# A recurrence step: the gates' weighted sums on DVE, the candidate's products on GpSimd and sums on ACT, scaling and adding fused

## The chip, the cores and the metric

The kernel runs on one core of a Trainium2 chip. The metric is the device time of one execution in microseconds, lower is better. The core has five engines with instruction queues of their own, which meet through semaphores: TensorE (PE in the profile, with PEld for its weight loads), VectorE (DVE), ScalarE (ACT), GpSimd (POOL) and SyncE (SP), which issues the transfers. TensorE writes its results into PSUM; the other operands lie in SBUF.

## The reference

The whole program is a stack of four residual layers over x of (2, 512, 128), each a conditioning block and a feed-forward block. The change lies in one of them, the conditioning block of layer 1: a gated recurrent unit with attention over a context of 77 tokens, run over the 512 positions one after the other for both batches.

```python
def step(h, x_t):
    hid = jnp.broadcast_to(h[:, None, :], (Bn, Sn, Hn))
    combined = jnp.concatenate([hid, enc_hiddens], axis=2)
    score = jnp.tanh(jnp.einsum('bsk,kh->bsh', combined, W_att))
    score = jnp.einsum('bsh,h->bs', score, V_att[:, 0])
    attn = jax.nn.softmax(score, axis=-1)
    context = jnp.einsum('bs,bsh->bh', attn, enc_hiddens)
    inp = jnp.concatenate([x_t, context], axis=1)
    gz, gr, gh = jnp.split(inp @ Wi + b, 3, axis=1)
    rz, rr, rh = jnp.split(h @ Uh, 3, axis=1)
    z = jax.nn.sigmoid(gz + rz)
    r = jax.nn.sigmoid(gr + rr)
    hh = jnp.tanh(gh + r * rh)
    h_new = z * h + (1.0 - z) * hh
    return (h_new, h_new)
_, outs = jax.lax.scan(step, last_hidden, jnp.swapaxes(dec_seq, 0, 1))
```

There are three sums over the attention for each of the 128 hidden units: one for the gate z, one for the gate r and one for the candidate hh. Everything is float32, B = 2, S = 512, and the context has NC = 77 tokens.

## The kernel before

`l1_xcond` (line 570) computes the block. Hidden units lie on the 128 partitions. What doesn't depend on the state is made ahead of the loop: `gx` holds the inputs' part of the three gates for all positions, `stat` the context's part of the score, and `gc` the context tokens already multiplied by the three gates' weights, as (batch, gate, token), 2 x 3 x 77 on each partition. `hs` holds the states of all steps.

The loop over `s` (line 611) stands in a manual schedule: every engine gets its instructions in the order of the source, and the waits between engines are worked out from what is read and written. One step goes like this, each line for both batches:

- TensorE multiplies the state by the score's weights (`pu`, line 614) and by the gates' recurrent weights, which it adds to `pc` in PSUM (lines 615, 625, 626). Columns 0 to 5 of `pc` then hold z, r and the candidate of both batches, columns 6 and 7 the half of the candidate's recurrent part.
- DVE adds `pu` to `stat` (`x`, line 619), ACT takes the tanh (`th`, line 621), TensorE weighs it with `vrep`, so that each partition holds all 77 scores (line 623).
- DVE takes the negative maximum of the scores (`nm`, line 629), ACT the exponential with its sum (`e` and `se`, line 634; in the trace a second instruction reads the accumulator).
- DVE multiplies the three rows of `gc` by `e` (`pr`, line 635), 231 elements for each batch, inverts the sum (`ri`, line 637), sums all products over the tokens (`pre`, line 639, 462 elements to 6), scales by `ri` (line 640) and adds `pc` (line 641).
- ACT makes both gates by one tanh of half the argument (`zr`, line 643), then the candidate for each batch, where `pre` is the bias and the gate r the scale (`hh`, line 646).
- DVE turns z into `oz` and `zh` (lines 649 and 651), multiplies `zh` by the old state (line 652) and makes the new state, one operation a batch (line 654).

`gates_in` (line 603) starts the next step's `pc` on TensorE with the inputs' part. GpSimd has no instruction in the loop.

Of the kernel before, what the change touches and what calls it, by code (L numbers as in the profile page):

```python
# [10 lines left out]
F32 = mybir.dt.float32  # L11
U8 = mybir.dt.uint8
AF = mybir.ActivationFunctionType
ALU = mybir.AluOpType
AX = mybir.AxisListType
PSUM = bass.MemoryType.PSUM

P = 128
B = 2
# [3 lines left out]
NC = 77  # L23
# [142 lines left out]
def tile_kernel(ctx: ExitStack, tc: tile.TileContext, d, off, out, phases=PHASES):  # L166
    nc = tc.nc
    pe, act, dve, pool = nc.tensor, nc.scalar, nc.vector, nc.gpsimd
# [27 lines left out]
    def mm_tile():  # L196
        return ps_tile("mm")
# [7 lines left out]
    def big(tag, bufs=None):  # L205
        t = act2[-1].tile([P, NT * P], F32, tag=tag, name=tag, bufs=bufs)
        return t
# [9 lines left out]
    def tview(t):  # L217
        return t.rearrange("p (t d) -> p t d", d=P)
# [12 lines left out]
    def col(name):  # L231
        a, n = off["cols"][name]
        return cols[:, a : a + n]
# [8 lines left out]
    def stage(*names):  # L242

        first = order.index(names[0])
        for k in order[:first]:
            weights.pop(k, None)
        load(order[: first + W_SLOTS])
        return parts(*names)
# [38 lines left out]
    def ln(src, dst, n=P, k=NT):  # L287

        st = sm([P, NT, 6], "ln_st")
        mv = sm([P, NT, 2], "ln_mv")  # L290
        for t in range(k):
            dve.bn_stats(st[:n, t, :], src[:n, t, :])
        for t in range(k):
            dve.bn_aggr(mv[:n, t, :], st[:n, t, :])
        r = rsqrt(mv[:n, :k, 1], n)
        for t in range(k):
            dve.tensor_scalar(dst[:n, t, :], src[:n, t, :], mv[:n, t, 0:1], r[:n, t : t + 1], ALU.subtract, ALU.mult)  # L297

    def transpose_to(dst, src, scale=None, bias=None):

        for b in range(B):
            ps = tr_tile()
            for i in range(TB):
                pe.transpose(ps[:, i * P : (i + 1) * P], src[:, b * TB + i, :], ident)
            o = dst[:, b * S : (b + 1) * S]
            if scale is None:
                act.copy(o, ps)
            elif bias is None:
                dve.tensor_scalar(o, ps, scale(b), None, ALU.mult)  # L309
            else:  # L310
                dve.tensor_scalar(o, ps, scale(b), bias(b), ALU.mult, ALU.add)

    def bcast(ap, shape, axis):
        return ap.unsqueeze(axis).to_broadcast(shape)
# [255 lines left out]
    def l1_xcond():  # L570
        w = stage("w1x")
        with tc.tile_pool(name="r1", bufs=1) as r1, tc.tile_pool(name="rs", bufs=3) as rs:
            y = tview(big("Y"))
            ln(X, y)
            yT = big("YT")
            transpose_to(yT, y)

            gx = r1.tile([P, S, 4, B], F32, tag="gx", name="gx")
            pool.memset(gx[:, :, 3, :], 0.0)
            for g in range(3):  # L580
                for b in range(B):
                    ps = mm_tile()
                    mm(ps, w("wi_x")[:, g * P : (g + 1) * P], yT[:, b * S : (b + 1) * S])
                    act.activation(gx[:, :, g, b], ps, AF.Identity, bias=col("gru_b")[:, g : g + 1])
            vrep = r1.tile([P, P], F32, tag="vrep", name="vrep")
            dve.tensor_copy(vrep, col("V_att").to_broadcast([P, P]))
            uhh = r1.tile([P, P], F32, tag="uhh", name="uhh")
            dve.tensor_scalar(uhh, w("uh")[:, 2 * P :], 0.5, None, ALU.mult)
            hs = r1.tile([P, S + 1, B], F32, tag="hs", name="hs")
            dve.tensor_copy(hs[:, 0, :], col("cond"))  # L590
            n2 = B * NC

            stat = r1.tile([P, B, NC], F32, tag="stat", name="stat")
            ps = mm_tile()
            mm(ps[:, :n2], w("wbot"), ctxT)
            act.copy(stat, ps[:, :n2].rearrange("p (b n) -> p b n", b=B))
            gc = r1.tile([P, B, 3, NC], F32, tag="gc", name="gc")
            for g in range(3):
                ps = mm_tile()
                mm(ps[:, :n2], w("wi_c")[:, g * P : (g + 1) * P], ctxT)  # L600
                act.copy(gc[:, :, g, :], ps[:, :n2].rearrange("p (b n) -> p b n", b=B))

            def gates_in(s):

                pc = o_tile()[:, :8]
                mm(pc, ident, gx[:, s].rearrange("p g b -> p (g b)"), start=True, stop=False)
                return pc

            with tc.manual_schedule():
                pc = gates_in(0)  # L610
                for s in range(S):
                    h = hs[:, s, :]
                    pu = mm_tile()[:, :B]
                    mm(pu, w("wtop"), h)
                    mm(pc[:, 0:2], w("uh")[:, :P], h, start=False, stop=False)
                    pb = []
                    for b in range(B):
                        x = rs.tile([P, NC], F32, tag="x", name="x")
                        dve.tensor_scalar(x, stat[:, b, :], pu[:, b : b + 1], None, ALU.add)  # L619
                        th = rs.tile([P, NC], F32, tag="th", name="th")  # L620
                        act.activation(th, x, AF.Tanh)  # L621
                        t = tr_tile()[:, :NC]
                        mm(t, vrep, th)
                        pb.append(t)
                    mm(pc[:, 2:4], w("uh")[:, P : 2 * P], h, start=False, stop=False)
                    mm(pc[:, 4:8].rearrange("p (c b) -> p c b", b=B), uhh, bcast(h, [P, 2, B], 1), start=False, stop=True)
                    nm = rs.tile([P, B], F32, tag="nm", name="nm")
                    for b in range(B):
                        dve.reduce_max(nm[:, b : b + 1], pb[b], axis=AX.X, negate=True)  # L629
                    e = rs.tile([P, B, NC], F32, tag="e", name="e")  # L630
                    se = rs.tile([P, B], F32, tag="se", name="se")
                    pr = rs.tile([P, B, 3, NC], F32, tag="pr", name="pr")
                    for b in range(B):
                        act.activation(e[:, b, :], pb[b], AF.Exp, bias=nm[:, b : b + 1], accum_out=se[:, b : b + 1])  # L634
                        dve.tensor_tensor(pr[:, b], gc[:, b], bcast(e[:, b, :], [P, 3, NC], 1), ALU.mult)  # L635
                    ri = rs.tile([P, B], F32, tag="ri", name="ri")
                    dve.reciprocal(ri, se)
                    pre = rs.tile([P, B, 3], F32, tag="pre", name="pre")
                    dve.tensor_reduce(pre, pr, AX.X, ALU.add)  # L639
                    dve.tensor_tensor(pre, pre, bcast(ri, [P, B, 3], 2), ALU.mult)  # L640
                    dve.tensor_tensor(pre, pc[:, 0:6].rearrange("p (g b) -> p b g", b=B), pre, ALU.add)  # L641
                    zr = rs.tile([P, B, 2], F32, tag="zr", name="zr")
                    act.activation(zr, pre[:, :, 0:2], AF.Tanh, scale=0.5)  # L643
                    hh = rs.tile([P, B], F32, tag="hh", name="hh")
                    for b in range(B):
                        act.activation(hh[:, b : b + 1], pc[:, 6 + b : 7 + b], AF.Tanh, bias=pre[:, b, 2:3], scale=zr[:, b, 1:2])  # L646
                    pcn = gates_in(s + 1) if s + 1 < S else None
                    oz = rs.tile([P, B], F32, tag="oz", name="oz")
                    dve.tensor_scalar(oz, zr[:, :, 0], -0.5, 0.5, ALU.mult, ALU.add)
                    zh = rs.tile([P, B], F32, tag="zh", name="zh")  # L650
                    dve.tensor_scalar(zh, zr[:, :, 0], 0.5, 0.5, ALU.mult, ALU.add)
                    dve.tensor_tensor(zh, zh, h, ALU.mult)
                    for b in range(B):
                        dve.scalar_tensor_tensor(hs[:, s + 1, b : b + 1], hh[:, b : b + 1], oz[:, b : b + 1], zh[:, b : b + 1], ALU.mult, ALU.add)  # L654
                    pc = pcn
            for b in range(B):
                ps = tr_tile()
                for i in range(TB):
                    pe.transpose(ps[:, i * P : (i + 1) * P], hs[:, 1 + i * P : 1 + (i + 1) * P, b], ident)
                ts_ = slice(b * TB, (b + 1) * TB)  # L660
                dve.tensor_tensor(X[:, ts_, :], X[:, ts_, :], tview(ps), ALU.add)
# [860 lines left out]
```

## Time and profile before

| What | Value |
|---|---|
| median of 3 runs | 6121.79 us |
| lowest and highest run | 6116.77 and 6127.82 us |
| the profiled execution: its own time | 6117.5 us |
| the profiled execution: its span | 6115.7 us |
| busy over the span: TensorE, DVE, ACT, POOL | 4296.3, 3110.0, 2092.1, 176.0 us |
| first and last `hs` of the loop start at | 265.5 and 3282.0 us |
| granted TensorE clock from 1000 to 2000 us | 0.50 |

The profile belongs to one execution. Its page has the span in equal slices, the chain that ended last and the costliest groups of instructions; the trace behind it can be asked for a stretch of time or for the instructions on one tile. In a row of the groups stand the line, the engine, the operation, the tiles as output and inputs, the shape and the count; after the bar the busy time in us and the mean duration in ns of one; after the second bar how long the engine was idle before these instructions, and who ended that. A line of a helper (215 is the helper of all matmuls) stands for many places, and then the tiles' names tell them apart.

### The profile page before, as it was taken

The page shows a single profiled execution, that of the slowest core. Times are in us where ns is not written, and L with a number is a line of the kernel's source. Part 1 is how long each engine was busy: PE and PEld are TensorE (multiplying, and loading weights), DVE is VectorE, ACT ScalarE, POOL GpSimd, SP SyncE. Part 2 cuts the span into 40 slices and gives each one's busy share as a digit, 9 for nine tenths or more (in the row PEclk, how much of TensorE's full clock was granted, in tenths as well). Part 3 has the DMA queues.
Part 4 walks back from the last instruction along what each step waited for, and adds up shares of the span by engine and source line. Part 5 has one row for each costly group of instructions (what it writes and reads, how often), then busy time and mean ns, then how long its engine had stood idle before and what let it go on. Part 6 is the DMA issues. An engine that isn't in the chain of part 4 may idle for free. (4 is left out here: it accounts for less than half of the span.)

```text
span 6115.7 us, 60242 instructions
## 1 busy us (share of the span) xinstructions
PE 4296.3 (70%) x19864; PEld 2898.0 (47%) x19864; DVE 3110.0 (51%) x10630; ACT 2092.1 (34%) x6050; POOL 176.0 (3%) x152
## 2 busy tenths in 40 slices
PE   4755555555555555555557999978888888888878
PEld 2655555555555555555555666833333333333334
DVE  6555555555555555555555444344444444444323
ACT  1433333333333333333333333314333333333322
POOL 2000000000000000000000000010000000000000
PEclk7855555555555555555556999779888888888866
DMA  1000000000000000000000000010000000000000
GB/s 37 26 1 1 1 1 1 1 0 1 1 1 1 1 0 1 1 1 1 1 1 15 21 1 5 1 42 7 6 18 6 18 6 18 6 20 7 7 4 6
DMA packets 15847, 44.43 MB, mean 7 GB/s; under 512 B 4179, under 2 KB 7965, under 8 KB 13869
## 3 DMA queue, kind: packets, MB, share of 16 engines
q1 hardware_dynamic: 15533, 40.57, 2.5%
q8 instruction: 157, 2.57, 0.2%
q14 instruction: 157, 1.29, 0.1%
HBM read 28.26 MB, written 0.52 MB: 5 GB/s over the span
## 5 line engine op out<-in xcount | busy, mean ns | idle before, releaser
L215 PE MATMUL mm<-hs,w1x 128*128 128x2 f32 x1024 | 299.9, 362 | 1204.2 <-DVE hs L654 1204.2
L215 PEld LDWEIGHTS mm<-hs,w1x 128*128 128x128 f32 x1024 | 255.9, 310 | 1252.5 <-DVE hs L654 1249.1
L1230 DVE TENSOR_REDUCE nm<-st 128x2 f32<-128x1024 f32 x384 | 462.5, 1223 | 418.1 <-PE st L215 417.6
L1236 ACT ACTIVATE pT<-st 128x1024 f32<-128x1024 f32 x384 | 389.0, 1023 | 815.2 <-PE st L215 794.7
L215 PE MATMUL tr<-th,vrep 128*128 128x77 f32 x2048 | 580.6, 436 | 120.1 <-ACT th L621 120.1
L215 PEld LDWEIGHTS o<-hs,w1x 128*128 128x128 f32 x2048 | 559.1, 333 | 0.0
L215 PEld LDWEIGHTS tr<-th,vrep 128*128 128x128 f32 x2048 | 473.9, 321 | 164.2 <-ACT th L621 164.2
L215 PE MATMUL o<-hs,w1x 128*128 128x2 f32 x2048 | 549.6, 338 | 0.0
L215 PE MATMUL st<-kp,qp 31*128 31x512 f32 (+1 forms) x1600 | 494.9, 751 | 71.9 <-DMA kp<-q 60.3
L629 DVE TENSOR_REDUCE nm<-tr 128x1 f32<-128x77 f32 x1024 | 243.4, 238 | 571.5 <-PE tr L215 571.5
L215 PE MATMUL st<-qp,kp 32*128 32x512 f32 (+1 forms) x1600 | 485.4, 710 | 39.9 <-DVE nm L1230 36.5
L634 ACT ACTIVATE e<-tr,nm 128x77 f32<-128x77 f32 x1024 | 333.6, 326 | 464.7 <-DVE nm L629 458.9
L621 ACT ACTIVATE th<-x 128x77 f32<-128x77 f32 x1024 | 226.4, 268 | 653.6 <-DVE x L619 653.6
L635 DVE TENSOR_TENSOR pr<-gc,e 128x231 f32<-128x231 f32 x1024 | 409.7, 400 | 43.1 <-ACT e L634 0.9
L619 DVE TENSOR_SCALAR x<-stat,mm 128x77 f32<-128x77 f32 x1024 | 225.3, 263 | 358.7 <-PE mm L215 358.7
L643 ACT ACTIVATE zr<-pre 128x4 f32<-128x4 f32 x512 | 105.6, 206 | 823.2 <-DVE pre L641 823.2
L639 DVE TENSOR_REDUCE pre<-pr 128x6 f32<-128x462 f32 x512 | 324.6, 634 | 0.0
L646 ACT ACTIVATE hh<-o,pre,zr 128x1 f32<-128x1 f32 x1024 | 303.9, 347 | 17.8 <-ACT zr L643 0.2
L215 PE MATMUL o<-gx,ident 128*128 128x8 f32 x1024 | 293.8, 361 | 0.0
L215 PE MATMUL acc<-pT,va 128*32 128x512 f32 (+1 forms) x1600 | 283.4, 685 | 12.8 <-ACT pT L1236 9.7
L215 PE MATMUL o<-hs,uhh 128*128 128x4 f32 x1024 | 290.5, 354 | 0.0
L215 PEld LDWEIGHTS st<-kp,qp 31*128 31x128 f32 (+1 forms) x1600 | 152.9, 219 | 275.5 <-issue 203.4
(361 smaller groups left out, 6145.5 us busy)
## 6 DMA issues: line engine op xcount, KB each, us to landing
w3x<-in_w3x SPq DMA_DIRECT2D x6, 1664.0 KB
qp<-q SPq DMA_DIRECT2D x104, 64.0 KB
kp<-q SPq DMA_DIRECT2D x48, 64.0 KB
w1g<-in_w1g SPq DMA_DIRECT2D x1, 2560.0 KB
w2a<-in_w2a SPq DMA_DIRECT2D x1, 2176.0 KB
w2b<-in_w2b SPq DMA_DIRECT2D x1, 2176.0 KB
w3f<-in_w3f SPq DMA_DIRECT2D x1, 1940.0 KB
w0g<-in_w0g SPq DMA_DIRECT2D x1, 1760.0 KB
```

The costliest lines, as they stand in the source:

```text
L215: pe.matmul(o, lhsT, rhs, start=start, stop=stop)
L619: dve.tensor_scalar(x, stat[:, b, :], pu[:, b : b + 1], None, ALU.add)
L621: act.activation(th, x, AF.Tanh)
L629: dve.reduce_max(nm[:, b : b + 1], pb[b], axis=AX.X, negate=True)
L634: act.activation(e[:, b, :], pb[b], AF.Exp, bias=nm[:, b : b + 1], accum_out=se[:, b : b + 1])
L635: dve.tensor_tensor(pr[:, b], gc[:, b], bcast(e[:, b, :], [P, 3, NC], 1), ALU.mult)
L639: dve.tensor_reduce(pre, pr, AX.X, ALU.add)
L643: act.activation(zr, pre[:, :, 0:2], AF.Tanh, scale=0.5)
L646: act.activation(hh[:, b : b + 1], pc[:, 6 + b : 7 + b], AF.Tanh, bias=pre[:, b, 2:3], scale=zr[:, b, 1:2])
L1230: dve.reduce_max(nms[h, g][:, j0 : j0 + 2, 0, u], ps, axis=AX.X, negate=True)
L1236: act.activation(pT, ps, AF.Exp)
```

## The change

`pr` holds two gates' products instead of three, so DVE multiplies 2 x 77 elements a batch and sums 308. The candidate's row of `gc` is multiplied by `e` on GpSimd into a tile of its own, `prc`, one instruction a batch, and ACT sums it by a copy onto itself with an accumulator (`sc`), one copy a batch, placed after both exponentials. Scaling and adding are one operation of DVE for each batch (times `ri`, plus `pc`), where they were two operations over both batches. The candidate's value gets an operation of the same kind in the loop over the batches that makes `hh`.

```diff
-                    pr = rs.tile([P, B, 3, NC], F32, tag="pr", name="pr")
+
+                    pr = rs.tile([P, B, 2, NC], F32, tag="pr", name="pr")
+                    prc = rs.tile([P, B, NC], F32, tag="prc", name="prc")
                     for b in range(B):
                         act.activation(e[:, b, :], pb[b], AF.Exp, bias=nm[:, b : b + 1], accum_out=se[:, b : b + 1])
-                        dve.tensor_tensor(pr[:, b], gc[:, b], bcast(e[:, b, :], [P, 3, NC], 1), ALU.mult)
+                        dve.tensor_tensor(pr[:, b], gc[:, b, 0:2, :], bcast(e[:, b, :], [P, 2, NC], 1), ALU.mult)
+                        pool.tensor_tensor(prc[:, b, :], gc[:, b, 2, :], e[:, b, :], ALU.mult)
+                    sc = rs.tile([P, B], F32, tag="sc", name="sc")
+                    for b in range(B):
+                        act.activation(prc[:, b, :], prc[:, b, :], AF.Copy, accum_out=sc[:, b : b + 1])
                     ri = rs.tile([P, B], F32, tag="ri", name="ri")
                     dve.reciprocal(ri, se)
                     pre = rs.tile([P, B, 3], F32, tag="pre", name="pre")
-                    dve.tensor_reduce(pre, pr, AX.X, ALU.add)
-                    dve.tensor_tensor(pre, pre, bcast(ri, [P, B, 3], 2), ALU.mult)
-                    dve.tensor_tensor(pre, pc[:, 0:6].rearrange("p (g b) -> p b g", b=B), pre, ALU.add)
+                    pcb = pc[:, 0:6].rearrange("p (g b) -> p b g", b=B)
+                    dve.tensor_reduce(pre[:, :, 0:2], pr, AX.X, ALU.add)
+                    for b in range(B):
+                        dve.scalar_tensor_tensor(pre[:, b, 0:2], pre[:, b, 0:2], ri[:, b : b + 1], pcb[:, b, 0:2], ALU.mult, ALU.add)
                     zr = rs.tile([P, B, 2], F32, tag="zr", name="zr")
                     act.activation(zr, pre[:, :, 0:2], AF.Tanh, scale=0.5)
                     hh = rs.tile([P, B], F32, tag="hh", name="hh")
                     for b in range(B):
+                        dve.scalar_tensor_tensor(pre[:, b, 2:3], sc[:, b : b + 1], ri[:, b : b + 1], pcb[:, b, 2:3], ALU.mult, ALU.add)
                         act.activation(hh[:, b : b + 1], pc[:, 6 + b : 7 + b], AF.Tanh, bias=pre[:, b, 2:3], scale=zr[:, b, 1:2])
```

## The prediction

> **What bounds the kernel now.** I read the page's costliest groups first, then the table of stretches, then the timeline of one step of the recurrence. The first group is TensorE's first matmul of a step, and its idle time tells where the kernel waits:
>
> ```profile
> L215 PE MATMUL mm<-hs,w1x 128*128 128x2 f32 x1024 | 299.9, 362 | 1204.2 <-DVE hs L654 1204.2
> L643 ACT ACTIVATE zr<-pre 128x4 f32<-128x4 f32 x512 | 105.6, 206 | 823.2 <-DVE pre L641 823.2
> ```
>
> Each of the 512 steps starts with the state `hs` that the step before ended with, so no step overlaps another. From 1000 to 2000 us the stretch table gives DVE 588 us busy, PE 562, ACT 351 and POOL 0 of 1000: no engine is full, the chain through all of them is. The step from the matmul at 2001.48 to the next at 2007.38 lasts 5.90 us, and 512 x 5.90 = 3021 us is half the span. Its second half:
>
> ```profile
> 2003.75 0.33 ACT L634 ACTIVATE e<-tr,nm 128x77 f32<-128x77 f32 x1 [0.90 <-DVE nm L629]
> 2004.18 0.33 ACT L634 ACTIVATE e<-tr,nm 128x77 f32<-128x77 f32 x1
> 2004.20 0.83 DVE L635 TENSOR_TENSOR pr<-gc,e 128x231 f32<-128x231 f32 x2
> 2004.40 0.19 ACT L634 ACTIVATION_READ_ACCUMULATOR e<-tr,nm 128x1 f32 x1
> 2004.94 0.16 DVE L637 RECIPROCAL ri<-se 128x2 f32<-128x2 f32 x1
> 2005.06 0.63 DVE L639 TENSOR_REDUCE pre<-pr 128x6 f32<-128x462 f32 x1
> 2005.73 0.17 DVE L640 TENSOR_TENSOR pre<-pre,ri 128x6 f32<-128x6 f32 x1
> 2006.00 0.17 DVE L641 TENSOR_TENSOR pre<-o,pre 128x6 f32<-128x6 f32 x1
> 2006.20 0.21 ACT L643 ACTIVATE zr<-pre 128x4 f32<-128x4 f32 x1 [1.60 <-DVE pre L641]
> 2006.44 0.17 DVE L649 TENSOR_SCALAR oz<-zr 128x2 f32<-128x2 f32 x1 [0.27 <-ACT zr L643]
> 2006.44 0.59 ACT L646 ACTIVATE hh<-o,pre,zr 128x1 f32<-128x1 f32 x2
> 2006.51 0.16 DVE L651 TENSOR_SCALAR zh<-zr 128x2 f32<-128x2 f32 x1
> 2006.71 0.16 DVE L652 TENSOR_TENSOR zh<-zh,hs 128x2 f32<-128x2 f32 x1
> 2006.97 0.35 DVE L654 SCALAR_TENSOR_TENSOR hs<-hh,oz,zh 128x1 f32<-128x1 f32 x2
> 2007.38 0.59 PE L215 MATMUL mm<-hs,w1x 128*128 128x2 f32 x2 [2.34 <-DVE hs L654]
> ```
>
> The columns are start, duration, engine, line, operation, count. The reader should see three things. The second `pr` starts at 2004.63 (a narrower window splits the pair), just after the second `e` has its sum (2004.40 + 0.19). From there to `zr` all is DVE, one instruction behind the other. After `zr` the two `hh` overlap on ACT (0.34 to 0.35 each, 0.25 apart, 0.59 together) while DVE makes `oz` and `zh` beside them; then come the two `hs`, 0.13 apart.
>
> **The change, part by part.** Times are of the step above. A hand-off between engines costs 0.03 (`zr` ends 2006.41, `oz` starts 2006.44); a DVE instruction that waits for another result of DVE and for a second engine starts 0.10 after it (2005.90 to 2006.00); independent DVE instructions start 0.08 before the end of the one in front.
>
> *Products and sum shrink.* 128x231 takes 400 ns and the 128x6 product 166: 1.04 ns an element, so 128x154 takes 0.32. The second `pr` ends 2004.63 + 0.32 = 2004.95. The sum of 462 takes 0.634, that of 77 (L629) 0.238: 1.03 ns an element, so 308 take 0.475. It starts 0.03 after the product, at 2004.98, and ends 2005.46. The reciprocal (0.16) still fits under the product's end.
>
> *Scaling and adding.* L640 and L641 (0.17 each, the second 0.10 behind the first) become two fused operations, one a batch. The nearest row is the fused `hs`, 0.22 each, 0.14 apart. They start 0.10 after the sum: 2005.56 and 2005.70, and end 2005.92. `zr` starts 2005.95 where it was 2006.20: **0.25 gained**.
>
> *The candidate's part.* Two products on POOL, two ACT copies that also sum, each followed by a read of the accumulator, two more fused operations on DVE. The POOL rows nearest to the product:
>
> ```profile
> L1143 POOL TENSOR_TENSOR q<-q,rot 128x512 f32<-128x512 f32 x36 | 45.7, 1269 | 272.8 <-DVE q L1142 272.8
> L1143 POOL TENSOR_TENSOR q<-q,rot 128x154 f32<-128x154 f32 x6 | 3.1, 510 | 173.8 <-DVE q L1142 173.8
> ```
>
> That is 2.12 ns an element, so 0.35 for 77 (0.51, the 154 row, as upper bound). The products end by about 2004.6 and 2005.1. A copy with sum costs at most what `e` costs with its read, 2003.75 to 2004.16 = 0.41; the second ends by 2005.55, before ACT is wanted for `zr`. Were both products 0.51, it would end about 2005.7: still covered. Cost: nothing, hidden under DVE's sum and scaling; without that cover each 0.1 delays `zr` by 0.1.
>
> *The hand-over at the end.* The loop that made the two `hh` now has a fused operation on DVE ahead of each. In the built program's order of instructions the first waits for the ACT sum. The second waits for the ACT signal that the **first `hh`** gives; consistent with that, `oz`, which needs `zr`, and the first `hs`, which needs the first `hh`, have no ACT wait of their own any more. So DVE stands still behind this operation, with `oz`, both `zh` and both `hs` queued behind it, and the second `hh` cannot overlap the first. From `zr` at 2005.95: it ends 2006.16; first `hh` 2006.19 to 2006.54; second fused operation 2006.57 to 2006.79; second `hh` 2006.82 to 2007.16. On DVE `oz` starts 2006.57 + 0.14 = 2006.71, `zh` 2006.79 to 2006.95, its product 2006.98 to 2007.14, `hs` 2007.18 and 2007.31, end 2007.53. Before, the end was 2007.32. The tail grows from 2007.32 - 2006.20 = 1.12 to 1.58, **0.46 lost**. The fused operations are bounded by 0.12 apart (with 0.17 durations, L641's) and 0.22 apart (nothing overlapped); I take the `hs` row, as it is the same operation. Sum: 0.46 - 0.25 = +0.20 with roundings (ends 2007.53 against 2007.32), or +0.10 with the short ones.
>
> *DVE and POOL together.* Now both engines wait for the same `e` and read `gc` and `e` at one time. The trace has no two-input DVE product beside a POOL product. Nearest is a DVE scaling beside one:
>
> ```profile
> L282 DVE TENSOR_SCALAR rs_e<-ln_mv x59: 151/171/854, 7.5 to 5906.3; 128x4 f32<-128x4 f32 x40, 128x8 f32<-128x8 f32 x18, 77x2 f32<-77x2 f32 x1
> ```
>
> and the timeline where the 854 ns fell:
>
> ```profile
> 5887.35 1.26 POOL L1339 TENSOR_TENSOR A<-A,rows 128x512 f32<-128x512 f32 x1 [1.23 <-DVE y L297]
> ...
> 5887.78 0.85 DVE L282 TENSOR_SCALAR rs_e<-ln_mv 128x4 f32<-128x4 f32 x1
> ```
>
> An instruction of 0.17 took 0.85 and ended 0.02 behind POOL's: it was held. At 8.1 us the same line ran beside a POOL product in 0.17, so holding is not general. Bounds: nothing, or the whole first POOL product behind the first `pr`: 2004.20 + 0.32 + 0.35 = 2004.87, so the second `pr` starts 0.24 late. POOL starts 0.08 after DVE's signal in this trace, DVE 0.03, so DVE goes first and POOL's work is the one pushed; the held row finished 0.02 after POOL's end, though it needs more than that from its start, so much of the overhead overlaps. I take 0.03.
>
> [...]
>
> **Sum.** 512 x (0.20 + 0.03) = 118 us. The profiled execution took 6117.5 us in all (span 6115.7), so 6235; the median of the runs shown, 6121.8, lies 4 above it, so **6239 us**. TensorE keeps its granted clock (0.50 in this stretch), and other stages are untouched.
>
> **Rivals.** *POOL holds the second product:* +0.20 + 0.24 = 0.44 a step, 225 us, 6347 us. For: the 0.85 row. Against: that row is another operation, and the same line also ran unheld. If POOL's second product slips in ahead too, another 0.35: 6526 us.
>
> *The handover costs nothing (faster):* if the second fused operation in fact runs ahead of the first `hh`, the tail stays 1.12 and the 0.25 gain stands: 6121.8 - 128 = 5994 us. It decides once the second fused operation can start less than 0.25 later than it would without the wait, since then less is lost than gained. For: nothing in the arithmetic needs the wait, the two batches touch different elements. Against: the built program has it.
>
> *Nothing to see:* gain and loss cancel, which needs a tail of 1.37; only with operations far shorter than any row.
>
> **Chances.** Forecast with 0 to 0.1 of holding 0.68; POOL holds 0.22; both products ahead 0.02; faster 0.06; nothing 0.02. The range goes from the short fused operations, 6121.8 + 512 x 0.10 = 6173, with a little off for the rare, so 6175, to the held case with 15 us on top, 6362. The forecast's own range is 6175 to 6290. Runs of this kernel spread over 11 us, so 0.2% (12 us) is what can be told from no change: faster 0.06, same 0.02, slower 0.92.
>
> **What would show it.** Right: `zr` about 1.0 us after the last `pr` ends (it was 1.17); the second candidate operation 0.03 behind the first `hh`; the two `hh` no longer overlapping but 0.63 apart; `oz` after it, not 0.03 after `zr`; a period near 6.13. The holding shows as POOL products longer than 0.35 and a second `pr` that starts late or lasts over 0.32. Wrong: `hh` still 0.25 apart, `zr` waiting for an ACT copy or POOL, or a period under 5.9.

## The result, and the profile after

The changed kernel takes 6207.34 us (median of 4 runs, 6205.4 to 6209.22), the kernel before beside it 6120.44 (6116.77 to 6127.82): 1.014 times as long, 95% interval 1.0123 to 1.0158, or 87 us more. The forecast was 6239 in a range of 6175 to 6362. On the chip of e1 to e4 (the experiments below) the runs of the kernel before, of e3 and of e4 fell on two levels about 40 us apart; their profiles are of the lower level, their medians and ratios are of all runs.

The rows of the last operation of a step give the length of a step in the profiled executions: `hs` starts from 265.5 to 3282.0 us before, from 266.3 to 3376.1 after, 511 steps each, so 5.90 and 6.09 us; 0.183 more in each of 512 is 94 us. The span grew by 89.5 (6115.7 to 6205.2), as what follows the loop became 4.6 us shorter. The page's groups of the changed kernel (busy time and mean ns of one, then idle time and its end) show the same first wait, 94 us longer, and the new POOL product:

```profile
L215 PE MATMUL mm<-hs,w1x 128*128 128x2 f32 x1024 | 300.0, 363 | 1298.2 <-DVE hs L662 1298.2
...
L638 POOL TENSOR_TENSOR prc<-gc,e 128x77 f32<-128x77 f32 x1024 | 464.7, 468 | 2664.0 <-ACT e L636 2664.0
```

The timeline of the changed kernel, second half of a step (start, duration, engine, line, operation, count, and in brackets the idle time before it and who ended it):

```profile
2003.58 0.75 DVE L637 TENSOR_TENSOR pr<-gc,e 128x154 f32<-128x154 f32 x2
2003.62 0.91 POOL L638 TENSOR_TENSOR prc<-gc,e 128x77 f32<-128x77 f32 x2 [5.17 <-ACT e L636]
...
2004.36 0.48 DVE L646 TENSOR_REDUCE pre<-pr 128x4 f32<-128x308 f32 x1
...
2004.73 0.19 ACT L641 ACTIVATION_READ_ACCUMULATOR prc<-prc 128x1 f32 x1
2004.94 0.34 DVE L648 SCALAR_TENSOR_TENSOR pre<-pre,ri,o 128x2 f32<-128x2 f32 x2
2005.20 0.21 DVE L653 SCALAR_TENSOR_TENSOR pre<-sc,ri,o 128x1 f32<-128x1 f32 x1
2005.32 0.20 ACT L650 ACTIVATE zr<-pre 128x4 f32<-128x4 f32 x1 [0.40 <-DVE pre L648]
2005.56 0.35 ACT L654 ACTIVATE hh<-o,pre,zr 128x1 f32<-128x1 f32 x1
2005.94 0.21 DVE L653 SCALAR_TENSOR_TENSOR pre<-sc,ri,o 128x1 f32<-128x1 f32 x1 [0.53 <-ACT hh L654]
2006.07 0.16 DVE L657 TENSOR_SCALAR oz<-zr 128x2 f32<-128x2 f32 x1
2006.14 0.16 DVE L659 TENSOR_SCALAR zh<-zr 128x2 f32<-128x2 f32 x1
2006.19 0.35 ACT L654 ACTIVATE hh<-o,pre,zr 128x1 f32<-128x1 f32 x1 [0.28 <-DVE pre L653]
...
2006.53 0.35 DVE L662 SCALAR_TENSOR_TENSOR hs<-hh,oz,zh 128x1 f32<-128x1 f32 x2
```

Two spans tell the story. From the first `pr` to `zr` it was 2006.20 - 2004.20 = 2.00 us, now 2005.32 - 2003.58 = 1.74: 0.26 gained. From `zr` to the end of `hs` it was 1.12, now 2006.88 - 2005.32 = 1.56: 0.44 lost. The brackets say where: DVE idles 0.53 until the first `hh` ends, then ACT idles 0.28 until the second fused operation ends. The two `hh` lie 0.63 apart (0.25 before), and `oz` and `zh`, which only need `zr`, stand in the queue behind the waiting operation.

### The profile page after: what moved, and what is told of

Read it like the earlier page. It is cut to its first block, busy times and chain, and to the rows that moved or that the text cites. A ratio compares the mean times of both kernels' runs of the same rounds, so it can differ in the third digit from the quotient of the medians.

```text
span 6205.2 us, 63827 instructions
## 1 busy us (share of the span) xinstructions
PE 4295.5 (69%) x19864; PEld 2897.1 (47%) x19864; DVE 3082.7 (50%) x11654; ACT 2516.3 (41%) x8098; POOL 640.8 (10%) x1176
## 5 line engine op out<-in xcount | busy, mean ns | idle before, releaser
L638 POOL TENSOR_TENSOR prc<-gc,e 128x77 f32<-128x77 f32 x1024 | 464.7, 468 | 2664.0 <-ACT e L636 2664.0
L654 ACT ACTIVATE hh<-o,pre,zr 128x1 f32<-128x1 f32 x1024 | 359.5, 351 | 165.5 <-DVE pre L653 146.7
L637 DVE TENSOR_TENSOR pr<-gc,e 128x154 f32<-128x154 f32 x1024 | 327.8, 320 | 83.4 <-ACT e L636 0.9
L653 DVE SCALAR_TENSOR_TENSOR pre<-sc,ri,o 128x1 f32<-128x1 f32 x1024 | 217.7, 213 | 274.9 <-ACT hh L654 274.3
L641 ACT ACTIVATE prc<-prc 128x77 f32<-128x77 f32 x1024 | 274.9, 268 | 118.4 <-POOL prc L638 0.3
```

Of the source, the lines that this page charges most:

```text
L637: dve.tensor_tensor(pr[:, b], gc[:, b, 0:2, :], bcast(e[:, b, :], [P, 2, NC], 1), ALU.mult)
L638: pool.tensor_tensor(prc[:, b, :], gc[:, b, 2, :], e[:, b, :], ALU.mult)
L641: act.activation(prc[:, b, :], prc[:, b, :], AF.Copy, accum_out=sc[:, b : b + 1])
L653: dve.scalar_tensor_tensor(pre[:, b, 2:3], sc[:, b : b + 1], ri[:, b : b + 1], pcb[:, b, 2:3], ALU.mult, ALU.add)
```

## The experiments

Step lengths below are worked out from the `hs` rows as above. A ratio compares an experiment with runs of the kernel before on the same chip.

**e1: both fused operations of the candidate ahead of both `hh`.** Against the changed kernel:

```diff
-                    for b in range(B):
-                        dve.scalar_tensor_tensor(pre[:, b, 2:3], sc[:, b : b + 1], ...)
-                        act.activation(hh[:, b : b + 1], ...)
+                    for b in range(B):
+                        dve.scalar_tensor_tensor(pre[:, b, 2:3], sc[:, b : b + 1], ...)
...
+                    for b in range(B):
+                        act.activation(hh[:, b : b + 1], ...)
```

> The two fused operations for the candidate stand together behind the gates' ones, ahead of both hh. Theory (the second one's wait for the first hh costs the tail): zr stays about 1.74 us after the first pr starts, the hh overlap again 0.25 apart, the tail from zr to the end of hs falls from 1.57 to 1.13, a step is 5.90 - 0.26 = 5.64 us, the kernel 6120 - 132 = 5988 us. Rival (the added instructions on DVE or the sharing with POOL cost it, not the wait): still 6150 to 6210 us.

Measured: 6012.79 us, ratio to before 0.9809 (0.9775 to 0.9842), a step 5.70 us. The loss is gone and the gain stands, 25 us less of it than expected: the tail is 2008.26 - 2007.07 = 1.19, where 1.13 was expected. Timeline of e1:

```profile
2006.95 0.33 DVE L652 SCALAR_TENSOR_TENSOR pre<-sc,ri,o 128x1 f32<-128x1 f32 x2
2007.07 0.20 ACT L650 ACTIVATE zr<-pre 128x4 f32<-128x4 f32 x1 [0.39 <-DVE pre L648]
...
2007.40 0.59 ACT L655 ACTIVATE hh<-o,pre,zr 128x1 f32<-128x1 f32 x2
...
2007.85 0.41 DVE L663 SCALAR_TENSOR_TENSOR hs<-hh,oz,zh 128x1 f32<-128x1 f32 x2
```

The two `hh` are 0.59 together again. But the first starts 0.33 after `zr`, where it was 0.24: in the built program it now waits for the *second* fused operation (2006.95 + 0.33 = 2007.28), though it reads only what the first wrote. It starts 0.12 behind that operation, where a hand-off took 0.03, so the wait alone does not account for all of it. A wait that moves with the order (of DVE for the first `hh` in the changed kernel, 0.53 idle; of ACT for the second fused operation here) and that the arithmetic doesn't need pointed the author to something that both engines use; e2 tests at what.

**e2: the order of the changed kernel, but the fused operations read a copy.**

```diff
                     dve.reciprocal(ri, se)
+                    pcs = rs.tile([P, B], F32, tag="pcs", name="pcs")
+                    dve.tensor_copy(pcs, pc[:, 4:6])
...
-                        dve.scalar_tensor_tensor(pre[:, b, 2:3], sc[:, b : b + 1], ri[:, b : b + 1], pcb[:, b, 2:3], ALU.mult, ALU.add)
+                        dve.scalar_tensor_tensor(pre[:, b, 2:3], sc[:, b : b + 1], ri[:, b : b + 1], pcs[:, b : b + 1], ALU.mult, ALU.add)
```

> The order of the changed kernel, but DVE copies the candidate's two columns of pc out of PSUM right behind the reciprocal, and the fused operations read the copy; then the second one has no wait for the first hh any more. Theory (it is this wait, and it comes from both engines reading one PSUM tile): the tail is 1.13 again and a step 5.59 to 5.66 us (the copy costs about 0.02; the first fused operation may start 0.07 earlier, as it waits for one engine less): 5962 to 5998 us. Rival (the place of the operation between the two hh costs, with the wait or without): about 6207 us.

Measured: **5946.15 us**, ratio to before 0.9701 (0.9668 to 0.9733), a step 5.57 us; it beats both kernels and lies 16 us below the range that was expected. Timeline of e2:

```profile
2002.10 0.75 DVE L637 TENSOR_TENSOR pr<-gc,e 128x154 f32<-128x154 f32 x2
...
2002.83 0.14 DVE L645 COPY pcs<-o 128x2 f32<-128x2 f32 x1
2002.89 0.47 DVE L648 TENSOR_REDUCE pre<-pr 128x4 f32<-128x308 f32 x1
...
2003.39 0.34 DVE L650 SCALAR_TENSOR_TENSOR pre<-pre,ri,o 128x2 f32<-128x2 f32 x2
2003.65 0.34 DVE L655 SCALAR_TENSOR_TENSOR pre<-sc,ri,pcs 128x1 f32<-128x1 f32 x2
2003.77 0.20 ACT L652 ACTIVATE zr<-pre 128x4 f32<-128x4 f32 x1 [0.33 <-DVE pre L650]
...
2004.01 0.59 ACT L656 ACTIVATE hh<-o,pre,zr 128x1 f32<-128x1 f32 x2
...
2004.54 0.35 DVE L664 SCALAR_TENSOR_TENSOR hs<-hh,oz,zh 128x1 f32<-128x1 f32 x2
```

Nothing of the arithmetic or of the order in the loop differs but one copy more and where two values are read from, and the tail is 2004.89 - 2003.77 = 1.12 again. DVE's idle 0.53 and ACT's 0.28 are gone once the fused operations don't read `pc` in PSUM: `hh` reads its columns 6 and 7, the fused operations of the changed kernel 4 and 5. The wait did not come from `pre`, which both engines still share as before. Whether it has to be one tile, or any read of PSUM on both engines is enough, no run shows. The second gain is in front: the gates' operations start 0.03 after the sum (2003.36 to 2003.39) where it was 0.10 (2004.84 to 2004.94), which fits a copy that has already waited for TensorE (e8 comes back to it). The expectation had allowed for these 0.07 at the candidate's first operation, and for 0.02 of the copy, which put the sum off by 0.01 only (0.79 behind the first `pr` for 0.78).

**e3: the hand-over alone, on the kernel before.**

```diff
-                    dve.tensor_tensor(pre, pre, bcast(ri, [P, B, 3], 2), ALU.mult)
-                    dve.tensor_tensor(pre, pc[:, 0:6].rearrange("p (g b) -> p b g", b=B), pre, ALU.add)
+                    pcb = pc[:, 0:6].rearrange("p (g b) -> p b g", b=B)
+                    for b in range(B):
+                        dve.scalar_tensor_tensor(pre[:, b, 0:2], pre[:, b, 0:2], ri[:, b : b + 1], pcb[:, b, 0:2], ALU.mult, ALU.add)
...
                     for b in range(B):
+                        dve.scalar_tensor_tensor(pre[:, b, 2:3], pre[:, b, 2:3], ri[:, b : b + 1], pcb[:, b, 2:3], ALU.mult, ALU.add)
                         act.activation(hh[:, b : b + 1], ...)
```

> The kernel before with the hand-over alone: all products and sums on DVE as before, no POOL and no ACT sums, but the gates scaled and added by one fused operation a batch, and the candidate's inside the hh loop. Theory: zr starts 0.02 earlier, the tail is 1.57 for 1.13, together +0.42 us a step, 6120 + 213 = 6333 us. Rival (POOL or the ACT sums are part of the loss): under 6200 us.

Measured: the profiled execution took 6333.54 us, the median of all four is 6352.82, ratio 1.0376 (1.0329 to 1.0422), a step 6.32 us, +0.42. Without POOL and without ACT sums the whole loss is there, in the same two idle times:

```profile
2004.06 0.35 ACT L648 ACTIVATE hh<-o,pre,zr 128x1 f32<-128x1 f32 x1
2004.44 0.21 DVE L647 SCALAR_TENSOR_TENSOR pre<-pre,ri,o 128x1 f32<-128x1 f32 x1 [0.53 <-ACT hh L648]
...
2004.69 0.35 ACT L648 ACTIVATE hh<-o,pre,zr 128x1 f32<-128x1 f32 x1 [0.28 <-DVE pre L647]
```

**e4: fused scaling and adding alone, on the kernel before.** The first five lines of e3's edit, with all three columns in one operation a batch.

> The kernel before with scaling and adding fused alone, three columns for each batch. By the changed kernel's rows (0.10 behind the sum, 0.13 apart, 0.21 long: 0.45, against 0.47 for the two operations before) 0.02 us a step are gained: 6120 - 11 = 6109 us. Rival (fusing is where the 0.26 of the first half came from): below 6050 us.

Measured: 6106.13 us, ratio 0.997 (0.9946 to 0.9994), a step 5.88 us. So of the 0.26 gained ahead of `zr` the fusing is 0.02, and the rest is the smaller products and sum (0.08 of the second product, 0.16 of the sum, by their rows).

**e5: e1 with the candidate's products on DVE.** `pr` has three rows again, POOL's product goes, and ACT sums from `pr[:, b, 2, :]`.

> As e1, but DVE makes the candidate's products too (231 elements a batch again) and ACT sums them from there; no POOL in the loop. Theory (POOL's part is worth the shorter pr alone): the last pr ends 0.08 us later, so 41 us above e1, about 6029 us. Rival (POOL and DVE disturb each other): equal to e1 or faster.

Measured: 6051.37 us, ratio to its own runs of before 0.9891 (0.9875 to 0.9908), a step 5.78 us against 5.70 of e1: 0.083, or 42 us. The 6029 expected had been reckoned from what e1 was expected to take, not from what it took, and was missed by 22; the difference to e1 came as expected. POOL's part is worth what it takes off DVE's product, and by this costs the path nothing.

**e6: POOL's products beside the sum, not beside DVE's products.**

```diff
-                        pool.tensor_tensor(prc[:, b, :], gc[:, b, 2, :], e[:, b, :], ALU.mult)
+                    for b in range(B):
+                        pool.tensor_tensor(prc[:, b, :], gc[:, b, 2, :], pr[:, 1, 0, :], ALU.mult)
```

> Both POOL products read the second batch's pr in place of e, so that the candidate's sums are not those of the reference; they start when both DVE products are done and run beside the sum, which reads one operand. Theory A (POOL was held by DVE's two-input product, so 0.46 to 0.48 is stretched): a POOL product takes 0.35 us. Theory B (0.46 is its own price): 0.42 to 0.48 us. The sums come later, so zr and the whole are later too: 6300 to 6410 us.

Measured, from the instructions on the tile (min, median and max ns):

```profile
L639 POOL TENSOR_TENSOR prc<-gc,pr x1024: 320/338/353, 262.2 to 3373.8; 128x77 f32<-128x77 f32 x171
```

So 0.32 to 0.35 is the price beside the sum, and the 423 to 483 ns of the changed kernel are stretched: theory A. The sum and POOL both read `pr` here, so a shared tile alone, beside an operation with one operand, didn't stretch it (median 0.338). The time, 6215.12 us (one run), missed the expectation by far: the sums end at about the moment when `zr` can start, so the delay came to almost nothing (a step takes 6.09 us, as in the changed kernel).

How much is stretched shows in the changed kernel, in narrow windows that split the pairs:

```profile
2003.62 0.46 POOL L638 TENSOR_TENSOR prc<-gc,e 128x77 f32<-128x77 f32 x1 [5.17 <-ACT e L636]
2004.00 0.32 DVE L637 TENSOR_TENSOR pr<-gc,e 128x154 f32<-128x154 f32 x1
```

DVE's first product ends at 2003.90. POOL's runs beside it for 0.28 and takes 0.12 longer than e6's median of 0.34, so it is not stopped for the whole overlap. By its record it ends at 2004.08; the second `pr`, which starts 0.08 before that, still takes 0.32.

**e7: a POOL product that starts first.** In the kernel before:

```diff
+                    du = rs.tile([P, B * 3 * NC], F32, tag="du", name="du")
+                    pool.tensor_tensor(du, gc.rearrange("p b g n -> p (b g n)"), nm[:, 0:1].to_broadcast([P, B * 3 * NC]), ALU.mult)
                     e = rs.tile([P, B, NC], F32, tag="e", name="e")
```

> The kernel before with one more POOL product of 462 elements a step, started by the first nm, so that it runs when DVE's pr starts; nobody reads it. Theory A (two-input products of DVE and POOL exclude each other, the later one waits): pr of the first batch lasts or starts until POOL's end, 0.4 to 0.9 us later, 6300 us or more. Theory B (they share): pr stays 0.40 us, POOL's takes about 1.16 us, the kernel 6120 us. Theory C (POOL alone gives way): pr stays 0.40, POOL's product takes up to 1.9 us, the kernel 6120 us.

Measured: 6304.63 us (one run), a step 6.26 us. The timeline in a window that splits the pair of `pr`:

```profile
2001.36 0.96 POOL L631 TENSOR_TENSOR du<-gc,nm 128x462 f32<-128x462 f32 x1 [5.30 <-DVE nm L629]
...
2001.77 0.81 DVE L637 TENSOR_TENSOR pr<-gc,e 128x231 f32<-128x231 f32 x1
```

`pr` takes 0.81 for 0.40 and ends 0.26 after POOL: it was held. That is theory A, though for part of the overlap only (0.41 longer, of 0.55 beside POOL's product). With e6: of the two products it was the later one that took longer, here `pr`, in the changed kernel POOL's (0.42 to 0.48 for 0.32 to 0.35). Of the 0.36 that a step grew, 0.29 lies at the two `pr`; the other 0.07 lies ahead of `nm`, which starts 1.00 after DVE's last work where it was 0.93, so the match with "6300 us or more" is in part another cost. In both kernels the two products also share `gc`; no run parts that from their having two operands each.

**e8: the copy alone, on the kernel before.** All six columns of `pc` are copied behind the reciprocal, and the adding reads the copy.

> The kernel before, but the six columns of pc are copied out of PSUM right behind the reciprocal, and the adding reads the copy. Theory (an instruction that waits for two engines starts 0.10 us behind the one in front, one that waits for a single signal 0.035): the adding starts 0.07 us earlier, the copy puts the sum off by 0.01 to 0.02, so 0.05 us a step, 26 us: 6094 us. Rival (the 0.10 belongs to reading PSUM, or the gain of e2 was the copy's for another reason): 6120 us or more.

Measured: 6090.45 us, ratio 0.9963 (0.9949 to 0.9977), a step 5.84 us, 0.06 less.

```profile
2003.71 0.17 DVE L642 TENSOR_TENSOR pre<-pre,ri 128x6 f32<-128x6 f32 x1
2003.91 0.17 DVE L643 TENSOR_TENSOR pre<-pcs,pre 128x6 f32<-128x6 f32 x1
```

The adding starts 0.03 behind the scaling, where it was 0.10. In the kernel before, the profile has one more row on DVE's queue for the adding, an `EVENT_SEMAPHORE`, 512 times; in e8 it has none. Alone e8 can't part the second wait from the read of PSUM, as both go; e2 can, since its gates' operations still read `pc` in PSUM and start 0.03 behind the sum. So the instruction with the second wait starts some 0.07 later in the kernel before, and moving that wait to an instruction off the path won 0.06 us a step.

## Why the prediction was right, and where its size was off

- *Products and sum.* `pr` 0.32 and the sum 0.476 were forecast to within 0.001, and `zr` started 0.26 earlier where 0.25 was said.
- *The candidate's part hidden.* Right: the second sum is read by 2004.92, `zr` starts 2005.32. A product took 0.42 to 0.48 and not 0.35, inside the bound of 0.51.
- *The hand-over.* Right, in every item that was named: the second fused operation 0.03 behind the first `hh`, `oz` behind it, the `hh` 0.63 apart, the tail 1.56 (1.58 said). e3 shows it as a cause by itself, e1 and e2 remove it in two ways. The prediction took the wait from the built program and didn't say why it is there; e2 shows that it hangs on DVE's read of `pc` in PSUM (with the copy the two idle times are gone and the tail is 1.12). What makes reads of different columns wait for each other, no run shows.
- *DVE and POOL together.* The mis-sized term: 0.03 a step (15 us) was taken, DVE paid nothing. In the changed kernel DVE's product starts 0.04 before POOL's, its 0.32 is unstretched, the second starts 0.42 after the first (0.43 before), and POOL's product is the one that grows. It grew by 0.12 of the 0.28 that it ran beside DVE's, and the second `pr` was not held by the last 0.08 of POOL's. Where POOL's product started first (e7), `pr` was the one that grew, by 0.41. So the 0.24 of the held case did not come here.
- *The sum.* 118 us were said. Less 15 for the holding, less 9 for the rest of the step (0.183 for 0.20), less 4 for the stages outside the loop makes 90, the growth of the span; the medians differ by 87. All three errors lie on the same side.
- *The rivals.* The faster one asked for a second fused operation that does not wait; with its wait gone in e2 the 0.26 did stand, and 0.07 on top. The held one did not come: POOL's first product had 0.08 to go when the second `pr` of the changed kernel started; in e7, where `pr` was held, POOL's had 0.55 to go.

## What to carry to other kernels

In this chain, which runs through all engines, the work taken off DVE gained only what the new hand-overs left: 0.26 us was won ahead of `zr` and 0.44 lost behind it. Look in the built program for waits that the arithmetic doesn't need; here ACT and DVE, which read different columns of one PSUM tile, were kept in turn (DVE idle 0.53, then ACT 0.28), and a small copy of 0.14 us out of PSUM, behind the reciprocal, removed both the turn and 0.07 of the start behind the sum (0.10 to 0.03). Of two products on DVE and POOL at the same time, the one that started later took longer here (POOL's 0.46 for 0.34, `pr` 0.81 for 0.40): try the order in which the one on the path starts first.

## What was not expected of the hardware

- The product that took longer was the one that started later. In the changed kernel DVE's starts 0.04 us ahead: DVE stayed at 0.32 and POOL took 0.42 to 0.48 (0.32 to 0.35 beside the sum, e6). In e7 POOL's starts 0.41 ahead: `pr` took 0.81 for 0.40. It ended 0.26 after POOL's product though it takes 0.40 alone, so by these rows part of it ran beside POOL's recorded time, as the second `pr` of the changed kernel did without growing (0.08 of it). e6 and e7 are one run each.
- The operations with an `EVENT_SEMAPHORE` row of 21 ns on DVE's queue (512 times each: the adding of the kernel before, the gates' fused operations of the changed one) start 0.10 us behind the instruction in front; with the copy out of PSUM (e8, e2) it is 0.03. That the 0.07 is the price of waiting for a second engine is the author's reading of these rows; over 512 steps e8 got 28 us from it by the medians.
